# Regrouping the graph columns and reordering the first routing batch in a graph layer followed by a two-of-eight expert layer

## The chip, the cores and the metric

The kernel runs on one core of a Trainium2 chip, in one launch. The metric is the device time of the launch in microseconds (us). Before the change four runs gave 506.99, 507.02, 508.55 and 510.12 us, with a median of 507.79 us.

## What is computed

There are 2048 tokens of 256 features, 67584 weighted edges between them, and eight experts. Everything is float32.

```python
xn  = layernorm(x)                                        # x: 2048 x 256
x   = x + segment_sum(edge_weight[:, None] * xn[dst], src) + node_vec1
xn2 = layernorm(x)
probs = softmax(xn2 @ Wr + br);  top_p, top_idx = top_k(probs, 2)
w   = top_p / top_p.sum()
y_e = gelu((xn2n * ln_g[e] + ln_b[e]) @ W1[e] + b1[e]) @ W2[e] + b2[e]   # xn2n: xn2 normalised again
x   = x + sum over the 2 chosen e of w_e * y_e
```

## The kernel before

**The graph layer.** The sparse sum is made dense. The 2048 columns of the weighted adjacency are cut into 16 column blocks of 128 (c0 to c15). In a loop over `n` from 0 to 31, each step makes half a column block: VectorE (DVE) builds one-hot matrices (`make_hots`, lines 306, 311 and 318, with a third part on GpSimd, also line 318), TensorE (PE) multiplies them (`make_cols`, line 343), ScalarE (ACT) copies the result out (line 346) and the queue of SyncE (SP) stores it to DRAM (line 347). After the second half of a block, SP loads the whole block back in another layout (line 350, buffer `ac`), and that load waits for both stores. The hots for step n+1 are issued in step n.

**Dense products.** `dense(cbs, b)` (line 352) multiplies, for the two row blocks b and b+1, the column blocks of one group `cbs` with the normalised tokens, into one of two PSUM buffers. One column block for two row blocks is called a unit here; it leaves four matmul records in the trace (float32 matmuls leave two each). `add` (line 361) adds the PSUM buffer to `acc` on DVE; for the first group it is three instructions (lines 367 and 369), for the others one (line 364). The groups are cut by `CS` (line 73), which was (2, 3, 4, 4, 3). Columns of the groups alternate between two pools of `max(CS)` = 4 buffers. A budget written by hand paces the dense products in the loop: from step 8 on, every step gains 3.5 units (line 501) and issues as many dense products as the budget holds (line 502); the last step issues all that remain but the last group's eight. So the first group is due from step 8 on. In step 29 DVE also copies a count of used edges (`used_i`, line 557), for which it needs a small matmul that PE issues behind that step's dense product (line 556), and only then DVE makes the hots of step 31.

**The tail of the graph layer.** After the loop there is a branch that is not taken on this data (line 569), and SP issues weight loads for the first three expert slots (lines 917 to 920). Then the last group's eight dense products, called D0 to D7 here, run with their adds A0 to A7 and, after each add, two sums of squares on ACT (line 670). At most two are in flight, because there are two PSUM buffers. Once row blocks 0 to 9 are final (after A4), routing of the first batch starts between the remaining ones: `roots` (lines 684 and 685, ACT), `scales` (690 to 697), `logits` (702, 703), `best` twice (711 to 719), `count` (726 to 734: marks `sel`, `seen_b` and the running totals `seen_t`), `sum_counts` (740 to 747: eleven matmuls into `pc`, which gives every token its place in its expert's list, and one into `all`, the totals), `shares` (752, 753: a difference on DVE and an Exp on ACT), an ACT instruction that brings the Sqrt table back (line 1079), and `choose` (806 to 812: a small `pos` and two large one-hot halves `chosen`, each for five row blocks). `choose` picks the rows of the first 256-row slot of expert 0.

**Behind the tail.** `set_shares` (758 to 761) finishes the first batch's records and stores them, `places` (767 to 777) and `enlist` (786 to 792) make one-hots of places on DVE, `choose_rows` (line 819, 40 matmul records) gathers the first slot's rows by a matmul with `chosen`, `scale_rows` (972) scales them on DVE, `list_rows` (line 800) multiplies the place one-hots on PE, and `layer_1` of the first expert slot (lines 998 and 1000) starts. From there on PE runs expert slots back to back.

**The order.** All this stands in sections in which the order of issue on each engine (but GpSimd's behind the loop) is the program's order; each engine runs its own queue in order, and the program's dependencies add the waits between engines.

The functions that the change touches, with their callers:

Of the kernel before, what the change touches and what calls it, by code (L numbers as in the profile page):

```python
# [26 lines left out]
def kernel(  # L27
# [42 lines left out]
    GB = P // GC  # L70
    GH = GB // 2
    QP = P // RK
    CS = (2, 3, 4, 4, 3)
    TS = 256
    TT = TS // P

# [275 lines left out]
    def dense(cbs, b):  # L352

        pa = ps_s.tile([P, 2, 512], F32, name="py1")
        for i in range(2):
            for c in cbs:
                nc.tensor.matmul(pa[:, i, :DX], acs[c][:, b + i, :], xn_sb[:, c, :],  # L357
                                 start=(c == cbs[0]), stop=(c == cbs[-1]))
        return b, pa, cbs[0] == 0

    def add(b, pa, first=False):

        if not first:
            nc.vector.tensor_add(acc[:, b:b + 2, :], acc[:, b:b + 2, :], pa[:, :, :DX])  # L364
            return
        for i in range(2):
            nc.vector.scalar_tensor_tensor(acc[:, b + i, :D], pa[:, i, :D], nv_c[:, b + i:b + i + 1],
                                           acc[:, b + i, :D], op0=OP.add, op1=OP.add)
        nc.vector.tensor_add(acc[:, b:b + 2, D:], acc[:, b:b + 2, D:], pa[:, :, D:DX])  # L369
# [247 lines left out]
    NA = 10  # L617
# [44 lines left out]
    with tc.manual_schedule(engines=ALL - {ET.Pool}):  # L662
# [5 lines left out]
        def square(b):  # L668
            sq = route.tile([P, D], F32, name="sq")
            nc.scalar.activation(sq, acc[:, b, :D], AF.Square, bias=less_m[:, b:b + 1], scale=1.0,  # L670
                                 accum_out=squares[:, b:b + 1])
# [7 lines left out]
        def roots(s):  # L679


            s["sd"] = sd2 = route.tile([P, 2, s["n"]], F32, name=f"sd2{s['i']}", bufs=1)
            sq = squares[:, s["b"]:s["b"] + s["n"]]
            nc.scalar.activation(sd2[:, 0, :], sq, AF.Sqrt, bias=eps_sb, scale=1.0 / D)
            nc.scalar.activation(sd2[:, 1, :], sq, AF.Sqrt, bias=eps2_sb, scale=(1.0 + EPS) / D)

        def scales(s):
            b0 = s["b"]
            s["r"] = r = route.tile([P, 2, s["n"]], F32, name=f"r{s['i']}", bufs=1)
            nc.vector.reciprocal(r, s["sd"])  # L690
            ms = route.tile([P, s["n"]], F32, name=f"ms{s['i']}", bufs=1)
            nc.vector.tensor_mul(ms, less_m[:, b0:b0 + s["n"]], r[:, 1, :])
            s["rec"] = rec = route.tile([P, s["n"], RW], F32, name=f"rec{s['i']}", bufs=1)
            for j in range(s["n"]):
                nc.scalar.activation(rec[:, j, :D], acc[:, b0 + j, :D], AF.Identity,
                                     bias=ms[:, j:j + 1], scale=r[:, 1, j:j + 1])
            nc.sync.dma_start(y_d[:N, :].rearrange("(b p) d -> p b d", p=P)[:, b0:b0 + s["n"], :],
                              acc[:, b0:b0 + s["n"], :D])

        def logits(s):  # L700
            s["z"] = z = route.tile(s["full"], F32, name=f"z{s['i']}", bufs=1)
            nc.vector.tensor_mul(z, acc[:, s["b"]:s["b"] + s["n"], D:], wide(s, s["r"][:, 0, :]))  # L702
            nc.vector.tensor_add(z, z, br_sb[:, None, :].to_broadcast(s["full"]))
            s["top"] = route.tile([P, 2, s["n"]], F32, name=f"top{s['i']}", bufs=1)
            s["hit"] = route.tile([P, s["n"], 2, NE], F32, name=f"hit{s['i']}", bufs=1)

        def best(s, i):

            top, hit, rec, z = s["top"], s["hit"], s["rec"], s["z"]
            io = iota_p[:, None, :NE].to_broadcast(s["full"])  # L710
            nc.vector.tensor_reduce(top[:, i, :], z, AX.X, OP.max)
            other = route.tile(s["full"], F32, name=f"other{s['i']}", bufs=1)
            nc.vector.tensor_tensor(other, z, wide(s, top[:, i, :]), OP.is_lt)
            nc.vector.scalar_tensor_tensor(other, other, float(NE), io, op0=OP.mult, op1=OP.add)
            nc.vector.tensor_reduce(rec[:, :, D + i], other, AX.X, OP.min)
            nc.vector.tensor_tensor(hit[:, :, i, :], io,
                                    rec[:, :, D + i:D + i + 1].to_broadcast(s["full"]), OP.is_equal)
            if i == 0:
                nc.vector.scalar_tensor_tensor(z, hit[:, :, 0, :], -3.0e38, z, op0=OP.mult,
                                               op1=OP.add)  # L720

        def count(s):

            hit = s["hit"]
            s["sel"] = sel = route.tile(s["full"], BF16, name=f"sel{s['i']}", bufs=1)
            nc.vector.tensor_add(sel, hit[:, :, 0, :], hit[:, :, 1, :])
            seen_b = route.tile([P, NE], BF16, name=f"seen_b{s['i']}", bufs=1)
            nc.vector.tensor_copy(seen_b, seen)
            s["seen"] = seen_b
            more = route.tile([P, NE], F32, name=f"more{s['i']}", bufs=1)  # L730
            nc.vector.tensor_reduce(more, sel.rearrange("p b e -> p e b"), AX.X, OP.add)
            nc.vector.tensor_add(seen, seen, more)
            s["seen_t"] = seen_t = route.tile([P, NE], BF16, name=f"seen_t{s['i']}", bufs=1)
            nc.vector.tensor_copy(seen_t, seen)

        def sum_counts(s):

            sel, seen_b = s["sel"], s["seen"]
            s["pc"] = pc = counts[:, s["i"], :s["n"], :]
            nc.tensor.matmul(pc, before, sel, start=True, stop=False)  # L740
            nc.tensor.matmul(pc, ones_b, seen_b[:, None, :].to_broadcast(s["full"]), start=False,
                             stop=False)
            for d in range(1, s["n"]):
                nc.tensor.matmul(pc[:, d:, :], ones_b, sel[:, :s["n"] - d, :], start=False,
                                 stop=(d == s["n"] - 1))
            s["all"] = counts[:, 2 + s["i"], 0, :]
            nc.tensor.matmul(s["all"], ones_b, s["seen_t"], start=True, stop=True)

        def shares(s):
            top = s["top"]  # L750
            s["odds"] = e = route.tile([P, s["n"]], F32, name=f"e{s['i']}", bufs=1)
            nc.vector.tensor_sub(e, top[:, 1, :], top[:, 0, :])
            nc.scalar.activation(e, e, AF.Exp)
# [46 lines left out]
                nc.tensor.matmul(listed[:, s["i"], :], in_lo[:, m, :], in_hi[:, m, :],  # L800
                                 start=(m == 0), stop=(m == n - 1))

        def choose(s):

            pos = route.tile([P, NA], F32, name="pos", bufs=1)
            nc.vector.scalar_tensor_tensor(pos, s["pc"][:, :, 0], 1.0, s["sel"][:, :, 0],
                                           op0=OP.add, op1=OP.mult)
            for h in range(2):
                j = slice(h * NA // 2, (h + 1) * NA // 2)
                n = [P, NA // 2, TS]  # L810
                nc.vector.tensor_tensor(chosen[:, j, :], pos[:, j, None].to_broadcast(n),
                                        place1[:, None, :].to_broadcast(n), OP.is_equal)
# [155 lines left out]
        def scale_rows(s, pt):  # L968
            ec = sets[s.set][3]
            xeT = heads[s.head][0]  # L970
            for k in range(KD):
                nc.vector.tensor_scalar(xeT[:, k, :], pt[:, k, :s.n * P], ec[:, KH + k:KH + k + 1],  # L972
                                        ec[:, KH + KD + k:KH + KD + k + 1],
                                        op0=OP.mult, op1=OP.add)
# [84 lines left out]
        NP = NB // 2  # L1059
        first_b, last_b = batch(0, 0, NA), batch(1, NA, NB - NA)  # L1060
        warm = route.tile([P, 1], F32, name="warm", bufs=1)
        late.append(dense(groups[-1], 0))
        for p in range(NP):
            if p + 1 < NP:
                late.append(dense(groups[-1], 2 * p + 2))
            add(*late.pop(0))
            square(2 * p)
            square(2 * p + 1)
            if p == NA // 2 - 1:
                roots(first_b)  # L1070
                scales(first_b)
                logits(first_b)
                best(first_b, 0)
            elif p == NA // 2:
                best(first_b, 1)
                count(first_b)
                sum_counts(first_b)
                shares(first_b)
                nc.scalar.activation(warm, eps_sb, AF.Sqrt)
            elif p == NA // 2 + 1:  # L1080
                choose(first_b)
        gnn.close()
        ps_h = ctx.enter_context(tc.tile_pool(name="ps_h", bufs=3, space=PSUM))
        ps_y = ctx.enter_context(tc.tile_pool(name="ps_y", bufs=2, space=PSUM))
# [2 lines left out]
        roots(last_b)  # L1087
        enlist(first_b)
        pt = choose_rows(first_b)
        scale_rows(whole[0], pt)  # L1090
        list_rows(first_b)
        hT = layer_1(whole[0])
# [96 lines left out]
```

## Time and profile before

| what | value |
|---|---|
| median of four runs | 507.79 us |
| the profiled execution | 506.89 us |
| its span | 505.1 us |
| around the span (the difference) | 1.8 us |
| PE busy in the span | 458.4 us (91%) |
| DVE busy in the span | 273.1 us (54%) |
| ACT busy in the span | 183.8 us (36%) |
| GpSimd (POOL) busy in the span | 195.7 us (39%) |
| mean granted TensorE clock | 0.975 |

The profile is of one execution. Times in it are microseconds from the start of the span. A row of the timeline gives a start, a busy time, the engine, the line, the operation, the tile written and the tiles read, and how many instructions it joins; brackets at the end hold the idle time of the engine just before it and what ended that. SPq is the time at which SP issues a transfer, not the transfer. "issue" is idle time for which the profile shows no cause. The shares above are means over stages with different limits, so that what matters for a change is read from its own stage. A fall of 0.05 us or less between rows is the time between an end and the next start, and ends of matmuls are modelled.

### The profile page before, as it was taken

The numbers are of one execution on the slowest core, as the hardware profiler recorded it, in microseconds if no ns is written. First come the engines' busy times: TensorE is split into PE (matmuls) and PEld (weight loads), VectorE is DVE, ScalarE is ACT, GpSimd is POOL, SyncE is SP. The second block draws the span as 40 slices with busy tenths as digits, with TensorE's granted clock in tenths as the row PEclk, the third lists the DMA queues.
The fourth block names the chain that finished last, engine by engine and source line by source line (L and its number), as shares of the span: only waits on it lengthen the run. The fifth ranks groups of instructions, "written<-read, shape, count | busy, mean of one in ns | idle before, by whom it ended". The sixth has DMA issues, their size and how long they took to land.

```text
span 505.1 us, 12115 instructions
## 1 busy us (share of the span) xinstructions
PE 458.4 (91%) x4996; PEld 394.6 (78%) x4996; DVE 273.1 (54%) x621; ACT 183.8 (36%) x422; POOL 195.7 (39%) x158
## 2 busy tenths in 40 slices
PE   4968598899998999898999999999999999998992
PEld 3867477677787878786888788888888888887881
DVE  6999999999999941228837222223233221212111
ACT  2477633333333110039382333322233423333320
POOL 3579664464634330000242444443453344422231
PEclk9996979999999999999999999999999999999997
DMA  6126768787877756963513997997999667226520
GB/s 215 53 76 206 233 193 242 220 223 244 221 213 218 233 172 205 353 225 105 189 46 83 316 328 237 354 365 213 333 357 309 158 199 219 31 36 204 151 81 31
DMA packets 84356, 102.15 MB, mean 202 GB/s; under 512 B 8240, under 2 KB 74656, under 8 KB 82176
## 3 DMA queue, kind: packets, MB, share of 16 engines
q1 hardware_dynamic: 74832, 86.26, 53.6%
q0 software_dynamic: 7984, 13.91, 12.2%
q10 hardware_dynamic: 1472, 1.06, 0.7%
q8 instruction: 44, 0.72, 0.6%
q14 instruction: 24, 0.20, 0.1%
HBM read 75.18 MB, written 28.14 MB: 205 GB/s over the span
## 4 chain that ended last, share of the span: by engine, by line
PE 37%; DMA 13%; issue 3%; DVE 2%; ACT 1%; SPq 1%; POOL 0%; POOLq 0%; DVEq 0%; ACTq 0%
PE py L1012 16%; PE ph L998 15%; DMA xs<-xr_d,to_i 8%; PE py L357 3%; DMA y_d<-ys,to_i 2%; DMA out<-y_d 2%; PE px L963 1%; PE px L819 1%; DMA so_far<-out,to_i 1%; SPq L1156 1%; DMA out<-ys,to_i 0%; POOL out L1033 0%; DVE acc L364 0%; POOLq L1185 0%; ACT L1000 0%
## 5 line engine op out<-in xcount | busy, mean ns | idle before, releaser
L357 PE MATMUL py<-xn_sb,ac 128*128 128x264 f32 x512 | 121.7, 393 | 4.4 <-DVE acc L369 2.0
L998 PE MATMUL ph<-xeT,w 128*128 128x256 f32 (+1 forms) x576 | 121.3, 368 | 2.3 <-PEq L1143 1.5
L1012 PE MATMUL py<-w,hT 128*128 128x256 f32 x544 | 121.0, 379 | 0.0
L998 PEld LDWEIGHTS ph<-xeT,w 128*128 128x128 f32 x576 | 104.3, 190 | 16.6 <-issue 2.9
L357 PEld LDWEIGHTS py<-xn_sb,ac 128*128 128x128 f32 x512 | 95.7, 191 | 23.5 <-issue 3.6
L1012 PEld LDWEIGHTS py<-w,hT 128*128 128x128 f32 x544 | 101.8, 190 | 13.0
L1000 ACT ACTIVATE hT<-ph,ec 128x256 f32<-128x256 f32 (+1 forms) x144 | 66.2, 461 | 117.3 <-issue 62.3
L1020 POOL DMA_INDIRECT y_d<-ys,to_i x30 | 48.5, 1616 | 118.5 <-DVE ys L1015 87.8
L318 POOL TENSOR_TENSOR hr<-eq,w 128x1024 bf16<-128x1024 bf16 x32 | 61.2, 1913 | 76.3 <-DVE hr L318 63.3
L343 PE MATMUL pa<-hl,hr 128*32 128x128 bf16 x3072 | 58.6, 235 | 18.8 <-issue 9.2
L306 DVE TENSOR_TENSOR hl<-k,iota_t 128x4096 bf16<-128x4096 bf16 x32 | 73.0, 2281 | 0.9 <-PE pa L343 0.9
L343 PEld LDWEIGHTS <-hr 128*32 128x32 bf16 x3072 | 50.0, 104 | 29.8 <-issue 15.9
L972 DVE TENSOR_SCALAR xeT<-px,ec 128x256 f32<-128x256 f32 (+1 forms) x38 | 18.4, 526 | 79.2 <-PE px L963 78.2
L924 POOL DMA_INDIRECT xs<-xr_d,to_i x39 | 40.5, 1038 | 49.7 <-DVE z L702 37.4
L346 ACT COPY ar<-pa 128x512 f32<-128x512 f32 x64 | 36.3, 583 | 59.3 <-PE pa L343 49.1
L1015 DVE SCALAR_TENSOR_TENSOR ys<-py,wt,b2w 128x256 f32<-128x256 f32 x34 | 16.3, 483 | 72.0 <-PE py L1012 60.8
L364 DVE TENSOR_TENSOR acc<-acc,py 128x528 f32<-128x528 f32 x32 | 22.5, 702 | 32.4 <-PE py L357 32.2
L318 DVE TENSOR_TENSOR hr<-eq,w 128x2048 bf16<-128x2048 bf16 x32 | 39.1, 1222 | 0.6
L987 ACT ACTIVATE b2w<-b,wt 128x256 f32<-128x256 f32 x36 | 16.3, 500 | 33.6 <-DVE wt L985 27.7
L311 DVE TENSOR_TENSOR eq<-k,iota_t 128x1024 bf16<-128x1024 bf16 x32 | 21.8, 681 | 0.0
L670 ACT ACTIVATE sq<-acc,less_m 128x256 f32<-128x256 f32 x16 | 7.9, 497 | 32.4 <-DVE acc L364 32.4
L410 PEld LDWEIGHTS pa<-wc,ar 128*128 128x128 f32 x64 | 12.7, 303 | 3.1 <-ACT ar L404 2.9
(196 smaller groups left out, 305.8 us busy)
## 6 DMA issues: line engine op xcount, KB each, us to landing
w<-in_L_ffn_W SPq DMA_DIRECT2D x40, 1024.0 KB
ad<-ar SPq DMA_DIRECT2D x32, 512.0 KB
ac<-ad SPq DMA_DIRECT2D x16, 1024.0 KB
b<-in_L_ffn_b SPq DMA_DIRECT2D x20, 128.0 KB
out<-y_d SPq DMA_DIRECT2D x4, 512.0 KB
xr_d<-rec SPq DMA_DIRECT2D x1, 1300.0 KB
y_d<-acc SPq DMA_DIRECT2D x1, 1280.0 KB
acc<-in_x SPq DMA_DIRECT2D x2, 512.0 KB
```

What stands on the lines that cost most here:

```text
L306: nc.vector.tensor_tensor(hl.rearrange("p g (n t) -> p g n t", t=2), two(k2[:, 0], g, P), pair(P), OP.is_equal)
L311: nc.vector.tensor_tensor(eq.rearrange("p g (n t) -> p g n t", t=2), two(k2[:, 1], g, RK), pair(RK), OP.is_equal)
L318: return engine.tensor_tensor(hr[:, i0:i1].rearrange("p i g (n t) -> p (i g) n t", t=2), eq[:, None, :, :].to_broadcast([P, i1 - i0, GH, RK]),
L343: nc.tensor.matmul(pa[j * RK:(j + 1) * RK, m, :], hr[:, i, g, :], hl[:, g, :], start=(i == 0), stop=(i == 2), tile_position=(0, j * RK))
L346: nc.scalar.copy(ar[:, m0:m0 + 4, :], pa)
L357: nc.tensor.matmul(pa[:, i, :DX], acs[c][:, b + i, :], xn_sb[:, c, :], start=(c == cbs[0]), stop=(c == cbs[-1]))
L364: nc.vector.tensor_add(acc[:, b:b + 2, :], acc[:, b:b + 2, :], pa[:, :, :DX])
L924: nc.gpsimd.indirect_dma_start(out=(sets[s.set][0] if into is None else into)[:, t, :], out_offset=None, in_=(xr_d if rows is None else ro ...
L998: nc.tensor.matmul(ph, w1[:, k, c * P:(c + 1) * P], xeT[:, k, :], start=(k == 0), stop=(k == KD - 1))
L1000: nc.scalar.activation(hT[:, c, :s.n * P], ph, AF.Gelu, bias=ec[:, c:c + 1], scale=1.0)
L1012: nc.tensor.matmul(py, hT[:, c, t * P:(t + 1) * P], w2[:, c, :], start=(c == 0), stop=(c == KH - 1))
L1020: st = nc.gpsimd.indirect_dma_start(out=y_d[:, :], out_offset=bass.IndirectOffsetOnAxis(ap=tos[s.to][:, t:t + 1], axis=0), in_=ys, in_offs ...
```

## The change

The groups become 3, 3, 3, 3 and 4 column blocks. D0 and D1 are issued ahead as before, and D(p+2) is issued right behind A(p), before the squares. `count` is split into `mark` (`sel`, `seen_b`) and `count_all` (the totals), `sum_counts` into `sum_marks` (the eleven matmuls) and `sum_all` (the one for the totals). D7, the last dense pair, is now issued before `sum_marks`. A6 with its squares is issued between the two halves of `choose`; `count_all` and `shares` follow the second half, and `sum_all` follows `choose_rows`. The second batch calls `count` and `sum_counts` as before.

```diff
-    CS = (2, 3, 4, 4, 3)
+    CS = (3, 3, 3, 3, 4)
...
         def count(s):
 
+            mark(s)
+            count_all(s)
+
+        def mark(s):
             hit = s["hit"]
...
             s["seen"] = seen_b
+
+        def count_all(s):
+            sel = s["sel"]
             more = route.tile([P, NE], F32, name=f"more{s['i']}", bufs=1)
...
         def sum_counts(s):
 
+            sum_marks(s)
+            sum_all(s)
+
+        def sum_marks(s):
             sel, seen_b = s["sel"], s["seen"]
...
+        def sum_all(s):
             s["all"] = counts[:, 2 + s["i"], 0, :]
             nc.tensor.matmul(s["all"], ones_b, s["seen_t"], start=True, stop=True)
...
-        def choose(s):
+        def choose(s, between):
...
             for h in range(2):
+                if h == 1:
+                    between()
...
-        late.append(dense(groups[-1], 0))
-        for p in range(NP):
-            if p + 1 < NP:
-                late.append(dense(groups[-1], 2 * p + 2))
+        for p in range(2):
+            late.append(dense(groups[-1], 2 * p))
+
+        def finish(p):
+
             add(*late.pop(0))
+            if p + 2 < NP:
+                late.append(dense(groups[-1], 2 * p + 4))
             square(2 * p)
             square(2 * p + 1)
-            if p == NA // 2 - 1:
-                roots(first_b)
-                scales(first_b)
-                logits(first_b)
-                best(first_b, 0)
-            elif p == NA // 2:
-                best(first_b, 1)
-                count(first_b)
-                sum_counts(first_b)
-                shares(first_b)
-                nc.scalar.activation(warm, eps_sb, AF.Sqrt)
-            elif p == NA // 2 + 1:
-                choose(first_b)
+
+        for p in range(NA // 2):
+            finish(p)
+        roots(first_b)
+        scales(first_b)
+        logits(first_b)
+        best(first_b, 0)
+        finish(NA // 2)
+        best(first_b, 1)
+        mark(first_b)
+        sum_marks(first_b)
+        choose(first_b, lambda: finish(NA // 2 + 1))
+        count_all(first_b)
+        shares(first_b)
+        nc.scalar.activation(warm, eps_sb, AF.Sqrt)
+        finish(NA // 2 + 2)
...
         pt = choose_rows(first_b)
+        sum_all(first_b)
         scale_rows(whole[0], pt)
```

## The prediction

> **What bounds the kernel now.** I read the page first: PE is 91% busy, and the chain that ended last is mostly PE's expert slots. The change touches nothing behind the start of the first slot, so the question is when layer_1 first runs on PE (247.35 us); what follows it shifts as a whole. The chain of waits, read around that point (start, length, what):
>
> ```profile
> 213.27 13.60 PE py L357 x60
> 226.89 0.72 DVE acc L364
> ...
> 233.79 0.24 DVE sel L726
> ...
> 234.99 2.78 PE py L357 x12
> 237.77 3.63 PE px L819 x17
> 241.39 7.11 issue
> 248.51 1.28 ACT L1000
> ```
>
> PE sets the pace until A4 at 226.89, then the first batch's routing on DVE does, until the count matmuls let PE go on with D7 and choose_rows. The timeline of the same stretch gives the prices:
>
> ```profile
> 234.09 0.21 PE L740 MATMUL counts<-sel,before 128*128 128x80 bf16 x1 [1.90 <-DVE sel L726]
> 235.63 2.89 DVE L811 TENSOR_TENSOR chosen<-pos,place 128x1280 f32<-128x1280 f32 x2
> 237.18 0.21 ACT L753 ACTIVATE e<-e 128x10 f32<-128x10 f32 x1
> 243.97 1.49 DVE L792 TENSOR_TENSOR in_hi<-in_hi,tok 128x2560 f16<-128x2560 f16 x1
> 247.35 2.81 PE L998 MATMUL ph<-xeT,w 128*128 128x256 f32 x12
> 248.51 1.28 ACT L1000 ACT_TABLE_LOAD   x1 [7.11 <-issue]
> ```
>
> PE stood idle 1.90 us ahead of the counts; that is the stall which the new order can take away. Third, the end of the loop:
>
> ```profile
> 156.15 1.29 PE L343 MATMUL pa<-hl,hr 128*32 128x128 bf16 x78 [1.76 <-issue]
> 178.59 3.83 PE L357 MATMUL py<-xn_sb,ac 128*128 128x264 f32 x16
> 182.57 0.14 DVE L557 CAST used_i<-pa 1x1 int32<-1x1 f32 x1 [4.55 <-PE pa L556]
> 190.25 21.63 PE L357 MATMUL py<-xn_sb,ac 128*128 128x264 f32 x96
> 199.32 0.33 SPq L350 DMA_DIRECT2D ac<-ad  x1
> ```
>
> DVE waits 4.55 us in step 29 for PE, and only then makes the last hots, so PE's position at step 29 sets the end of the loop. The 96 records are the leftover of step 31. The last load of a column block, c15, goes out at 199.32.
>
> **The change, part by part.** No work is added or removed: 512 dense records, 40 adds and the same routing instructions on both sides. Only order and waits change.
>
> *Rate of dense work.* 96 records take 21.63 us and 16 take 3.83, so a record costs (21.63 - 3.83)/80 = 0.2225 us, a unit (four records) 0.89 us, and a run has 0.27 us behind its last record.
>
> *Leftover at step 31.* The budget gives 3.5 units in each of steps 8 to 31. Counted through line 502, the loop has issued 80 units before step 31 with the old groups and 78 with the new. Of 104 and 96 units due in the loop, 24 and 18 remain: the leftover shrinks by 6 x 0.89 = 5.34 us. The last group grows from 24 to 32 units, 7.12 us.
>
> *Where the loop ends.* Both groupings have done 48 units after step 21. Then the old one does 4, 4, 0, 4, 4, 4, 4, 4 and the new one 3, 3, 3, 6, 3, 3, 3, 3 up to step 29. A PE step is 5.21 us with four units (171.93 to 177.14) and 4.32 with three (113.14 to 117.46). The new step 25 can begin at about 154.7: its hots start on DVE at 147.8, or 0.6 later by the regrouped adds, and GpSimd's third is ready 6.3 us after. From there six units (1.45 for the column products, 5.34, 0.2) and four steps of 4.32 give 179.0 for the end of step 29, and `used_i` at 179.4. If the unexplained stall of 1.76 before 156.15 comes again, it is 181.2. Against 182.57 the loop ends 3.2 or 1.4 us earlier; I take the middle, **2.3**, since that stall is seen once near there and its cause isn't.
>
> *First group of three.* c2's load goes out at 64.77. The load of c8 went out at 128.21 and PE resumed on it at 134.20, so a load takes up to 5.9 us and c2 is there at 70.7. The first dense product, now at 68.14, will wait some 1.7 us, and DVE's first add as much. I count it as hidden: the old grouping puts two of the dear first-group adds (1.04 us each) into steps 9 to 11, the new one spreads them; by step 22 DVE is 0.6 late, as used above. Without that cover it costs up to 1.8.
>
> *Column loads and SP.* SP's order of transfers is unchanged. c7's load now needs c0's buffer, c13's c6's and c10's c3's; their last readers run in steps 14, 28 and 21, at about 104, 176 and 142, while SP reaches those loads at 119.85, 178.90 and 147.94: no new wait. SP paces itself on the stores' landings (110.1 of its wait between 64 and 200), so the loads don't move up with PE, beyond the 1.0 us that SP waits for ACT at step 31. c15 goes out at about 198.3 and is there at 204.2.
>
> *Start of D0 (T).* Before, T = 213.27: the leftover ends at 211.88, and 1.39 goes to the last add and the branch. After, T = 213.27 - 5.34 - 2.3 = 205.6. D0 reads c15 after six records, at 206.9, so c15 is in time by 2.7 us.
>
> *From T to layer_1.* Before: 247.35 - 213.27 = 34.1. After, with rows of the same instructions:
> - D0 to D7 without a gap: 128 x 0.2225 = 28.5. D7 needs A5, which ends 5.6 after A4's start, at T + 23.7, ahead of D7's turn at T + 24.9.
> - the eleven count matmuls behind D7 0.5, to `pos` 0.1: T + 29.1. `sel` is ready at T + 25.0 already; DVE idles 3.9 us. **The stall moves from PE to DVE.**
> - `pos` 0.26, half of `choose` 1.41, A6 0.61, other half 1.41, the totals 0.61, the difference 0.16: T + 33.5. A6 and the totals, 1.2 us that lay in front of `pos`, are now in the chain.
> - the Exp. ACT's table load at line 1000 started at 248.51, when the first product was there, though ACT was idle for 7.11 us: the load stands behind the wait. So after the difference come 1.28 + 0.21 and some 0.1: T + 35.1. A7 (0.61) runs beside it. Before, Exp ended 1.7 us ahead of line 758 and cost nothing: 1.0 us is new. If the load can run ahead, nothing is.
> - from line 758 to the end of `enlist`: 245.46 - 239.05 = 6.4: T + 41.5. choose_rows (8.8 from the first half's end at T + 30.9) is done at T + 39.8, hidden.
> - list_rows 1.3 and 0.1: T + 42.9, with scale_rows (1.0) beside it.
>
> So layer_1 starts 43.0 - 34.1 = 8.9 us later after T, and T is 7.6 us earlier: **+1.3 us**.
>
> *Costed at nothing.* D(p+2) ahead of the squares, and D0, D1 ahead: PE's and ACT's orders stay as they are. `sum_all` behind choose_rows (0.17): PE waits for `enlist` there; without that cover it costs its 0.17. The squares of A6 before Exp (1.3): over before the difference. The record store (line 761) goes out 1 us later, against a gather that begins at 248.96; the store lands near 247.5, so 1.4 us are left. GpSimd issues nothing differently.
>
> *A rule against the change.* The row first: between the end of the squares (235.86) and Exp (237.18) lies a table load of 1.28 and nothing else. The Trainium skill, "ScalarE: Activation LUTs", section "What ACT_TABLE_LOAD costs", says that a switch costs about 1.28 us plus about 1.38 us of drain. By the page the Exp step would cost 1.4 us more and the sum would be +2.7 (an estimate from that page); this trace shows no drain on the wait, and the sum goes by the trace.
>
> **How it stands to the median.** The profiled execution is 506.89 us, of which 505.1 are span. +1.3 makes 508.2. The median of the four runs is 0.9 above that execution, so that the same sum there makes 509.1. I forecast **508.5**, between the two.
>
> **Rivals.**
> 1. *No earlier end of the loop, slower.* The place is PE in steps 25 to 31: the six-unit step with the stall again, or a late c15 in D0. Each microsecond by which T is later than 205.6 adds one, since everything from D7 to `enlist` hangs on it. With no gain but the leftover T is 207.9 and the sum +3.6: 510.5 to 511.4. For c15 it decides when the load takes over 8.6 us, against 5.9. The weight loads queued behind it speak for it (380 GB/s from 202 to 204); c8, with two stores queued behind it, speaks against. Chance 0.27.
> 2. *The stall is really gone, faster.* `used_i` at 179.4 and an Exp table that doesn't wait: 8.9 - 1.0 - 5.34 - 3.2 = -0.6: 506.3 to 507.2. At the most T falls to the landing of c15 (204.2 - 1.3 = 202.9): -1.5, or -2.5 with no wait at Exp: 504.4 to 505.3. The 1.90 us idle before the counts speaks for it; that the counts then stand behind D7 speaks against. Chance of more than 0.5% faster 0.11.
> 3. *It doesn't do what it says.* The dense pair goes ahead, but the counts become the late thing. This is my forecast, +0 to +2.4 us: chance 0.62, with the near part of rival 2 in it.
>
> **Numbers.** 0.5% (2.5 us) is about what a measurement of this kernel can tell from no change. Slower by more than that, over 510.3, is rival 1 (0.27); faster, under 505.3, is the far part of rival 2 (0.11); 0.62 lie between. The likeliest case's own range is 507 to 510.3. The range of 8 in 10 takes in rival 1 to 511.5 and rival 2 to 506.0.
>
> **What would show it.** In the profile after: D0 near 205.6; 128 dense records to about T + 28.5 without a gap; an idle DVE of 3 to 4 us ended by line 744 ahead of `pos`; DVE at line 758 released by ACT's Exp; line 998 near 248.6. It is wrong if D0 waits for a column load, if `used_i` comes after 182, or if line 758 doesn't wait.

## The result, and the profile after

Over all runs made side by side the changed kernel took 510.10 us (median of 48 runs, 505.13 to 516.42), the kernel before 507.95 (median of 74, 503.49 to 515.08). The ratio is 1.0037, with a 95% interval of 1.0020 to 1.0055: slower by 1.9 us (1.0 to 2.8). That is less than the half per cent that the prediction took as about the least that can be told from no change, but with this many runs it is clear of zero. The forecast sum was +1.3, and the forecast median 508.5 with 507 to 510.3 for the likeliest case: the measured median lies inside, 0.2 us from the upper end.

The two profiles, one execution each:

| what | before | after |
|---|---|---|
| the profiled execution | 506.89 us | 510.03 us |
| its span | 505.1 | 508.3 |
| step 29's column products start | 177.14 | 179.40 |
| T, D0 starts | 213.27 | 209.29 |
| `pos` (line 806, now 819) | 235.37 | 238.34 |
| layer_1 starts (line 998, now 1013) | 247.35 | 251.03 |
| T to layer_1 | 34.08 | 41.74 |
| from layer_1 to the end of the span | 257.75 | 257.27 |

What follows layer_1 is the same within half a microsecond in this pair, as expected (in the other profiles it took 256.4 to 258.5 us). The tail grew by 7.66 us, and T came only 3.98 earlier in this pair. The chain of waits of the changed kernel, at the place where the chain of before went from A4 through the routing on DVE:

```profile
209.29 28.72 PE py L357 x128
...
240.09 0.63 DVE acc L364
...
240.80 1.09 ACT sq L670 x4
...
241.91 1.28 ACT L766
...
243.45 0.18 DVE both L771
...
246.44 5.74 issue
252.18 1.28 ACT L1015
```

All 128 records of D0 to D7 now stand in the chain, without a gap; before, it left the dense products after 60. From A6 (240.09) the chain goes through A6's squares on ACT and the table load in front of Exp to line 771 (758 before). The timeline behind them (start, busy time, engine, line, operation; idle time before it in brackets):

```profile
234.43 0.17 DVE L732 CAST seen_b<-seen 128x8 bf16<-128x8 f32 x1
...
237.92 0.39 PE L755 MATMUL counts<-sel,ones_b 128*128 128x72 bf16 x9
238.34 0.17 DVE L819 SCALAR_TENSOR_TENSOR pos<-counts,sel 128x10 f32<-128x10 f32 x1 [3.74 <-PE counts L755]
240.24 8.87 PE L834 MATMUL px<-chosen,rec 128*128 128x256 f32 x40 [1.93 <-DVE chosen L826]
241.91 1.28 ACT L766 ACT_TABLE_LOAD   x1
242.63 0.16 DVE L765 TENSOR_TENSOR e<-top 128x10 f32<-128x10 f32 x1
242.71 0.70 DVE L364 TENSOR_TENSOR acc<-acc,py 128x528 f32<-128x528 f32 x1
243.21 0.21 ACT L766 ACTIVATE e<-e 128x10 f32<-128x10 f32 x1
243.45 0.17 DVE L771 TENSOR_SCALAR both<-e 128x10 f32<-128x10 f32 x1
248.37 1.49 DVE L805 TENSOR_TENSOR in_hi<-in_hi,tok 128x2560 f16<-128x2560 f16 x1
249.91 1.28 PE L813 MATMUL listed<-in_hi,in_lo 128*128 128x128 f16 x20 [0.80 <-DVE in_hi L805]
251.03 2.81 PE L1013 MATMUL ph<-xeT,w 128*128 128x256 f32 x12
```

The marks are ready at 234.6. DVE then idles 3.74 us, because the count matmuls wait their turn behind D7. PE in turn idles 1.93 us for the first half of `chosen`, and waits again for `enlist` at line 813. The old stall of 1.90 us on PE is gone, and three others stand in its place. At 241.91 ACT's table load starts, 0.02 us behind A6's squares and before DVE has written `e` (242.63): it did not wait for `e`.

The loop of the changed kernel:

```profile
144.36 0.40 PE L343 MATMUL pa<-hl,hr 128*32 128x128 bf16 x8 [2.51 <-issue]
144.70 5.65 PE L357 MATMUL py<-xn_sb,ac 128*128 128x264 f32 x12
...
180.85 2.94 PE L357 MATMUL py<-xn_sb,ac 128*128 128x264 f32 x12
183.94 0.15 DVE L557 CAST used_i<-pa 1x1 int32<-1x1 f32 x1 [2.61 <-PE pa L556]
190.27 1.41 PE L343 MATMUL pa<-hl,hr 128*32 128x128 bf16 x88 [1.70 <-POOLq L569]
191.61 16.29 PE L357 MATMUL py<-xn_sb,ac 128*128 128x264 f32 x72
```

PE lost 2.51 us at 144 with no cause shown, and 12 records then took 5.65 us where they take 2.94 elsewhere; the granted clock was 0.50 from 144 to 150. `used_i` came at 183.94, later than the 182.57 of before, and step 31 waited 1.70 us for GpSimd, where before it waited 0.93:

```profile
188.91 1.41 PE L343 MATMUL pa<-hl,hr 128*32 128x128 bf16 x88 [0.93 <-POOLq L569]
```

The leftover is 16.29 us in place of 21.63: exactly the 5.34 that were counted.

Single executions differ: with the same groups, step 29 began up to 4.8 us apart. So the experiments below are read by stretches inside a profile as well as by ratios. Some executions of most of these kernels ran over 1.5% longer than the fastest of the same kernel; the ratios leave them out, the medians above do not, and of the profiles of e5 and e7, which were such executions, only stretches are used.

### The profile page after: what moved, and what is told of

The parts are those of the page before. It is cut to its first block, busy times and chain, and to the rows that moved or that the text cites. A ratio compares the mean times of both kernels' runs of the same rounds, so it can differ in the third digit from the quotient of the medians.

```text
span 508.3 us, 12113 instructions
## 1 busy us (share of the span) xinstructions
PE 462.4 (91%) x4996; PEld 395.5 (78%) x4996; DVE 273.2 (54%) x621; ACT 183.6 (36%) x422; POOL 192.7 (38%) x158
## 3 DMA queue, kind: packets, MB, share of 16 engines
q10 hardware_dynamic: 1472, 1.06, 0.6%
## 4 chain that ended last, share of the span: by engine, by line
PE 38%; DMA 12%; issue 3%; DVE 1%; ACT 1%; SPq 1%; POOL 0%; POOLq 0%; DVEq 0%; ACTq 0%
PE py L1027 16%; PE ph L1013 15%; DMA xs<-xr_d,to_i 8%; PE py L357 6%; DMA y_d<-ys,to_i 2%; DMA out<-y_d 1%; PE px L978 1%; DMA so_far<-out,to_i 1%; SPq L1178 1%; DMA out<-ys,to_i 0%; DVE chosen L826 0%; POOL out L1048 0%; POOLq L1207 0%; ACT L1015 0%; ACT L766 0%
## 5 line engine op out<-in xcount | busy, mean ns | idle before, releaser
L357 PE MATMUL py<-xn_sb,ac 128*128 128x264 f32 x512 | 124.7, 400 | 2.8 <-DMA ac<-ad 1.4
L357 PEld LDWEIGHTS py<-xn_sb,ac 128*128 128x128 f32 x512 | 97.3, 194 | 22.6 <-issue 2.3
L343 PE MATMUL pa<-hl,hr 128*32 128x128 bf16 x3072 | 59.9, 233 | 20.1 <-issue 7.7
L364 DVE TENSOR_TENSOR acc<-acc,py 128x528 f32<-128x528 f32 x32 | 22.3, 701 | 34.4 <-PE py L357 34.3
```

Of the source, the lines that this page charges most:

```text
L343: nc.tensor.matmul(pa[j * RK:(j + 1) * RK, m, :], hr[:, i, g, :], hl[:, g, :], start=(i == 0), stop=(i == 2), tile_position=(0, j * RK))
```

## The experiments

Theory O (order): the tail is slower because D7 stands ahead of the counts. Rival L (loop): the loss is in the loop. Ratios are to the kernel before on the same chip, with 95% intervals, 12 runs against 35.

**e1_groups_only.** Only the groups change; the old order stays.

```diff
-    CS = (2, 3, 4, 4, 3)
+    CS = (3, 3, 3, 3, 4)
```

> Only the groups become 3, 3, 3, 3, 4; the old order of the tail stays (counts ahead of D7, choose in one piece, totals with the counts). Theory O (order): the loss is that D7 stands ahead of the count matmuls, so that pos waits for it; from T, the start of D0, to the first product of layer_1 it was 34.1 us before and 41.7 after. Here A4 comes 4.5 us later after T than before, since five dense pairs have 16 records in place of 12, and the counts wait little for DVE; D7, 0.9 us longer, follows them. T to layer_1: 39.4 us, 2.3 less than after; ratio to before about 0.999. Rival L (loop): the loss is in the loop, where the groups of three end later than the shorter leftover promises, and the order of the tail is neutral: T to layer_1 near 41.7 and a ratio of 1.004 or more.

Measured: 0.9989 (0.9942 to 1.0036); T 208.66, T to layer_1 39.43 us. The stretch is the one that theory O named (39.4); rival L's 41.7 is out. The profile lists no idle time of PE ahead of the counts here.

**e2_order_only.** The new order with the old groups.

```diff
-    CS = (3, 3, 3, 3, 4)
+    CS = (2, 3, 4, 4, 3)
```

(against the changed kernel)

> Only the order of the tail changes; the groups stay 2, 3, 4, 4, 3. Theory O: with dense pairs of 12 records D7 is done 21.4 us after T, the marks at 20.5, so that pos comes where it came before (22 us after T); A6 and the totals (1.2 us) now lie behind pos, and half of that is hidden behind choose_rows: T to layer_1 34.7 us against 34.1 before, ratio 1.001. Rival L: the same or less than 34.1, ratio 1.000 or below. T itself as before, about 213, give or take what one execution differs from another.

Measured: 1.0004 (0.9967 to 1.0041); T 213.54, `pos` 22.56 us after T, T to layer_1 36.0. The stretch missed the expected 34.7 by 1.3 us. Two things are in that: D7 waited 0.37 us for A5, and choose_rows ran slowly:

```profile
236.10 0.17 DVE L819 SCALAR_TENSOR_TENSOR pos<-counts,sel 128x10 f32<-128x10 f32 x1 [1.71 <-PE counts L755]
238.00 10.56 PE L834 MATMUL px<-chosen,rec 128*128 128x256 f32 x40 [1.94 <-DVE chosen L826]
```

10.56 us in place of 8.87 for the same 40 records. The windows of this profile show why (PE busy, weight loads, DVE, ACT, POOL; then the granted clock, the DMA share and GB/s):

```profile
238.00:240.00 2.00, 2.00 (x7) 1.71 (x8) 2.00 (x3) 1.42 (x5) 0.00 (x0) 0.75 0.04 8
240.00:242.00 2.00, 2.00 (x6) 1.53 (x6) 1.82 (x9) 1.97 (x3) 0.00 (x0) 0.50 0.00 0
```

The granted clock fell to 0.50 behind the idle time of 1.94 us. Without these 1.7 us the stretch is 34.3, near the 34.1 of before: with short dense pairs the new order costs next to nothing. The ratio says the same.

**e3_counts_before_d7.** The changed kernel, with D7 issued behind the counts. `ahead(p)` is the part of `finish(p)` that issues D(p+2), here a function of its own; only the calls are shown.

```diff
-        finish(NA // 2)
+        finish(NA // 2, last=False)      # A5 and its squares, without D7
         best(first_b, 1)
         mark(first_b)
         sum_marks(first_b)
+        ahead(NA // 2)                   # D7
```

> The changed kernel, but the eleven count matmuls are issued ahead of D7 in place of behind it; the rest (groups, A6 between the halves of choose, totals behind them) stays. Theory O: pos comes 25.9 us after T in place of 29.1, DVE no longer idles 3.7 us ahead of it, and choose_rows behind D7 becomes the late thing: T to layer_1 39.5 us in place of 41.7, ratio to before about 0.999. Rival L: pos moves, but layer_1 doesn't (41 us or more), ratio 1.003 or more.

Measured: 0.9965 (0.9930 to 1.0000); T 207.57, `pos` 25.81 us after T, T to layer_1 39.05.

```profile
233.20 3.81 PE L357 MATMUL py<-xn_sb,ac 128*128 128x264 f32 x16
233.38 0.17 DVE L819 SCALAR_TENSOR_TENSOR pos<-counts,sel 128x10 f32<-128x10 f32 x1 [0.51 <-PE counts L755]
236.84 8.80 PE L834 MATMUL px<-chosen,rec 128*128 128x256 f32 x40
246.62 2.81 PE L1013 MATMUL ph<-xeT,w 128*128 128x256 f32 x12
```

D7 runs while DVE makes `chosen`, and choose_rows follows it without idle time. One moved call takes 2.7 us out of the stretch (41.74 in the changed kernel); this shows that D7 ahead of the counts is what costs in the tail. The ratio follows: that of the changed kernel itself, run beside it (e4, 1.0044), lies outside this one's interval. It fits theory O (39.5) and rules out rival L, that the order of the tail is neutral.

**e4_after_again.** The changed kernel itself, no edit.

> The changed kernel itself once more, for what differs between executions. Theory O: T to layer_1 41.7 us within 0.1, as that stretch is a fixed order with no transfer in it; T itself differs by microseconds (209.3 in the first profile, with 2.5 us of PE idle at 142 for which the profile shows no cause and half the granted clock until 150 behind it; without such a stall 205 to 206). Rival L: T near 209 again, with the loop late for the same reason at the same step.

Measured: 1.0044 (1.0005 to 1.0082); T 206.60, T to layer_1 41.73, against 41.74 in the first profile. The tail is a fixed stretch; T moves. PE's loss stood at 144 again, 2.51 us, but this time the clock stayed up, and `used_i` came at 181.25.

**e5_before_again.** The kernel before, no edit.

> The kernel before, once more. With groups of 2, 3, 4, 4, 3 T (the start of D0) was 213.27 and 213.54 us in two executions, and PE lost 1.76 and 1.75 us at 156 with no cause shown; with groups of 3 T was 206.6, 207.6, 208.7 and 209.3, and the losses stood at 144 and 174. Theory: the places of these losses belong to the grouping, so 156 again, and T 213 to 214; T to layer_1 34.1. Rival: they are chance of the execution, and come elsewhere, T differing by over 1 us. Ratio 1.000.

Measured: 1.0004 (0.9974 to 1.0035). In its profile PE's losses stood at 95, 135, 164 and 176, none at 156. So their places do not belong to the grouping alone; the theory as put is not shown. e8 below, with the old groups too, had none at 156 either. T to layer_1 was 35.76, with the clock at 0.51 between 240 and 242, behind PE's idle time ahead of the counts.

**e6_after_used_first.** The changed kernel, with the count of used edges ahead of step 29's dense product. e8 has the same edit on the kernel before.

```diff
             make_cols(n, *hots.pop(n))
+            if n == NH - 3:
+                used = small.tile([P, 1], F32, name="used", bufs=1)
+                nc.vector.tensor_reduce(used, used_q, AX.X, OP.add)
+                used_i = small.tile([1, 1], I32, name="used_i", bufs=1)
+                pu = ps_a.tile([P, 4, P], F32, name="pa")[:, 0, :1]
+                nc.tensor.matmul(pu, ones, used, start=True, stop=True)
+                nc.vector.tensor_copy(used_i, pu[0:1, :])
...
-            if n == NH - 3:
...
```

> The changed kernel, with the count of used edges in step 29 (reduce on DVE, a small matmul on PE, a copy on DVE) issued ahead of that step's dense product in place of behind it. Theory W: the regrouped loop doesn't end earlier because DVE waits 2.6 to 3.2 us for PE in step 29, so that the last hots and GpSimd's third come 1.7 us late for PE in step 31. Here DVE gets the count some 2.8 us sooner, PE's wait at step 31 (1.7 us) goes, T is 1.7 to 1.9 earlier than the 206.6 of the same kernel without a late stall (about 205 to 207), T to layer_1 stays 41.7, and the ratio to before is about 1.000 in place of 1.004. Rival: another limit (the load of the last column block, or GpSimd) keeps T where it was, ratio 1.004.

Measured: 0.9986 (0.9946 to 1.0027); T 209.54, T to layer_1 42.47 (the clock fell to 0.50 in choose_rows here too). In the one profile T is late, and outside the expected 205 to 207, since step 29 was: it began at 181.54. From there to T it took 28.00 us, against 29.89 to 29.91 in the four other profiles with groups of three and the old place of `used_i`. The 1.9 us are those of theory W, and PE's wait at step 31 is gone:

```profile
183.41 0.15 DVE L504 CAST used_i<-pa 1x1 int32<-1x1 f32 x1 [0.99 <-PE pa L503]
190.41 1.52 PE L343 MATMUL pa<-hl,hr 128*32 128x128 bf16 x96
191.86 16.29 PE L357 MATMUL py<-xn_sb,ac 128*128 128x264 f32 x72
```

**e8_before_used_first.**

> The kernel before with the count of used edges ahead of the dense product of step 29, nothing else. Theory W: here PE itself is the late one (its steps take 5.2 us against 4.7 of DVE), and only its 0.93 us wait for GpSimd's third at step 31 goes: T about 212.4, ratio 0.998. Rival: the gain is as large as with the groups of three (1.7 us or more), T 211.6 or less, ratio 0.996.

Measured: 0.9963 (0.9933 to 0.9993). T was 216.85 in a profile whose step 29 began at 181.62; from there to T 35.23 us, against 36.13, 36.13 and 36.14 in the three profiles of the old groups without this edit. That is the 0.9 of theory W. T itself missed the expected 212.4, since step 29 was late. The ratio is below the expected 0.998, which lies within its interval.

**e7_counts_and_used_first.** The edits of e3 and e6 together.

> Both mends together: counts ahead of D7, and the count of used edges ahead of the dense product of step 29. Theory: the two gains add, 2.7 us in the tail (T to layer_1 39.05) and 1.7 to 1.9 at the end of the loop: ratio to before 0.993, faster than both kernels. Rival: with T at 205 the last column block's load (there at about 204) or the first batch's marks set the pace again, and less than 3 us of the 4.5 remain against the changed kernel: ratio 0.998.

Measured: 0.9943 (0.9913 to 0.9974), faster than the kernel before and the changed one; the expected 0.993 lies inside the interval, the rival's 0.998 outside. The stretches are T to layer_1 39.06, and 28.09 from step 29 to T: both gains are there in full.

## Why the prediction was right, and where it was off

**Direction and size.** +1.3 us was forecast as a sum, +1.9 (1.0 to 2.8) was measured, and the likeliest case was the one that came: the dense pair goes ahead and the counts become late. The terms, though, were off by more than their sum: the tail was forecast 1.2 us too dear and T 1.5 us too early, and that these two cancel is luck. Of the three signs of being wrong that the prediction names, two came: `used_i` after 182 (183.94 in the first profile; 181.25 in e4), and a line 758, now 771, that did not wait.

**Tail, +8.9 forecast, +7.66 measured.** The counts: `pos` was put at T + 29.1 and came at T + 29.05; DVE's idle time at 3.9 us, measured 3.74 (`sel` was put at T + 25.0, where the rows of before give 25.2 and it came at 25.22); D0 to D7 without a gap, as said. From line 771 to the end of `enlist` 6.4, measured 6.41. The term that failed is the Exp: "the load stands behind the wait ... 1.0 us is new". The table load began at 241.91, 0.7 us before DVE started the difference. Exp ended at 243.42 and A7 at 243.41, and line 771 followed at 243.45, T + 34.2 in place of T + 35.1: the two paths ended together, so that neither the Exp nor A6's squares, behind which its load had to start, cost more than 0.01 us beyond DVE's own work. The other 0.3 us lie behind `enlist`: 1.17 us to layer_1, where 1.4 and a rounding had been added. The sign that misled was real (at line 1015 the load again began only at 252.18, after 5.74 us of idle time), but it does not hold for every load; what parts the two, no run here shows. The Trainium skill, "ScalarE: Activation LUTs", section "What ACT_TABLE_LOAD costs", adds 1.38 us of drain to a switch of tables. For this step it would have gone further wrong: the load started 0.02 us after A6's squares and Exp 0.02 us after the load's end.

**T, 7.6 us earlier forecast.** The shorter leftover gave its 5.34, exactly. The other 2.3 were to come from an earlier `used_i`. Of this, 0.89 is the dense product of step 29 itself, three units in place of four, and it is there: 29.90 from the start of step 29 to T against 36.13, a difference of 6.23 = 5.34 + 0.89. The other 1.4 did not come. Step 29 began at 177.14, 177.41 and 181.62 with the old groups (mean 178.7) and at 179.40, 178.76, 177.66, 176.70 and 181.54 with the new (mean 178.8): no gain in the means, though single values lie up to 4.8 us apart. The ratio agrees: +1.9 (1.0 to 2.8), less a tail of 7.66, leaves 4.9 to 6.7 us by which T came earlier, not 7.6. The step that failed is "The new step 25 can begin at about 154.7". In the five profiles it began at 156.06 to 159.59. In e4 it was 156.19, and PE had lost 2.51 us at 144, in step 22, with no idle time listed between:

```profile
144.12 0.29 PE L343 MATMUL pa<-hl,hr 128*32 128x128 bf16 x8 [2.51 <-issue]
156.19 1.52 PE L343 MATMUL pa<-hl,hr 128*32 128x128 bf16 x96
```

That loss (1.48 to 2.51) was in all five profiles, and in three of them a second of 0.94 to 2.53 followed near 174 to 178. One of 1.76 had been allowed for, as the upper of two bounds. So T is 6.1 us earlier by the means, and the sum 7.66 - 6.1 = +1.5, against +1.9 measured.

**What causes those losses is open.** The profile calls them "issue". The one at 144 came while the DMA engines were nearly full: busy share 1.06 from 142 to 144 in the first profile after and 0.88 in e4, with one packet of the instruction queue in each of the two windows beside it (140 to 142 and 144 to 146). In all five profiles the loss in step 22 stood at the same place, behind the 88th of the step's 96 matmul records. A late fetch of PE's instructions would fit, but such packets come about every 6 us in this stretch, so that one nearby proves little; no run took it apart.

**First group of three.** The wait for c2 was put at 1.7 us and counted as hidden. Five profiles show 0.5 to 2.7 us of PE waiting there. DVE's hots of step 18, counted from those of step 8, came after 53.2 to 54.2 us in three profiles of the old groups and after 52.9 to 54.7 in four of the new: hidden there, as said. In the fifth, e6, it was 57.6 us, with the longest wait for c2 (2.7) and 2.06 us of PE idle at 104 for which the profile shows no cause; how much of it the wait made is not shown.

**c15.** It went out at 198.09 (forecast 198.3), and D0 never waited for it, not even with T at 206.60 in e4. The first rival's second mechanism did not come. Its first, no earlier end of the loop, is the half of it that did: the 1.4 us. In the four profiles of the new groups other than e6 T was 206.60 to 209.29, mean 208.0, nearer to this rival's 207.9 than to the forecast's 205.6.

**Rival 2**, the stall really gone, is ruled out by the idle times above, and e3 shows what it would have taken.

## What to carry to other kernels

Work that fills one engine's wait must be shorter than that wait: PE idled 1.9 us ahead of the counts, and the dense pair put there was 3.56 us long, in front of eleven matmuls of 0.5 us on which everything hung. With longer pairs the wait was gone without the move: with the new groups and the old order (e1) the counts followed D6 with no idle time listed, so neither part of the change alone was measurably slower (0.9989 and 1.0004, each within some 0.4%), and the two together were (1.0037). Small results that another engine waits for belonged ahead of long work in PE's order of issue, in the tail (2.7 us) as in the loop (`used_i`, 1.9 us and 0.9 us).

## What the runs showed of the hardware that was not expected

An idle time of 1.93 or 1.94 us on PE ahead of choose_rows was followed by half the granted clock in two of four executions with the new order (e2: 1.7 us lost; e6: 0.7) and not in the other two (the first profile after, and e4: 8.87 us for the 40 records). The Trainium skill, "TensorE: Matmul & The Clock Gate", section "HAM oscillation — how this bites in real kernels", asks for no idle gap over some 3.4 us; here a gap of 1.9 us was enough at times. Without such a gap, in e1, e3 and e7, choose_rows took its 8.80 us each time. The 2.51 us of idle time at 144 did the same once (0.50 from 144 to 150 in the first profile after) and once not (1.00 throughout in e4).
